# A two-layer graph attention and mixture-of-experts kernel: gate logits of 16 tiles as VectorE dots, a written engine order from the last attention block on, a guessed weight ring, and packing in half-megabyte pieces

## The chip, the core and the metric

The kernel runs on one core of one Trainium2 chip. The metric is the device time of one execution in microseconds. Each of the core's engines has a queue of its own: TensorE (PE in the profile, PEld for its weight loads), VectorE (DVE), ScalarE (ACT), GpSimd (POOL) and SyncE (SP). Most plain DMAs are issued from SP's queue; indirect DMAs (gathers and scatters by a list of row numbers) are issued from POOL's.

## The reference

There are 2708 tokens of 256 features, and an adjacency matrix of 2708 x 2708 integers of which some 1.2% are one. Two layers follow each other, each with a graph attention and a mixture of eight experts of which each token uses two. Cut to what matters:

```python
# layer 0
xn = layernorm(x)
q, k, v = xn @ Wq.T + bq, xn @ Wk.T + bk, xn @ Wv.T + bv
scores = where(adj > 0, q @ k.T / 16, -9e15)
x = x + elu(softmax(scores) @ v)
xt = layernorm(x)
top_p, top_idx = top_k(softmax(xt @ Wr + br), 2)
weights = top_p / top_p.sum(-1)
xe = layernorm(xt) * ln_g[e] + ln_b[e]            # for each expert e
y[e] = gelu(xe @ W1[e] + b1[e]) @ W2[e] + b2[e]   # hidden 1024
x = x + sum over the two experts of weights * y[e]
# layer 1: attention from s_src[i] + s_dst[j], the same mask, then eight experts of hidden 512
```

## The kernel before

**Tiles and blocks.** Tokens are cut into 22 tiles of 128 (the last has 20). The attention of layer 0 runs over six blocks of queries: five of 512 queries (tiles 0 to 3, 4 to 7 and so on) and a last one of 148 (tiles 20 and 21). A block has 22 key steps. In each, `scores` multiplies a tile of keys with the block's queries (L545; L552, L578 and L584 for the rest of the columns and the mask of the left-over keys), ScalarE takes the exponential (L557), and VectorE multiplies it with the mask (L560). Three key steps later (`LAG`), `attend` adds these weights times the values into four accumulators, one for each tile of the block (L609).

**Masks.** The mask of the next block is built during the present one: a quarter tile of the adjacency matrix is loaded on SP's queue, VectorE compares it (L411) and transposes it (L417). The columns of the left-over keys are loaded and compared by `load_apart` (compare L432), called at key step 14 (at step 0 in the last block). Its result, `apart`, is needed by the matmuls of L552 and L584 in the last key steps of the same block. At a block's end its mask is written to DRAM (`neighbours`, 1.4 MB), to be read again in layer 1.

**Routing beside the attention.** When a block's attends are done, `evict` (L634) copies the four accumulators out, and a generator `finish` for each tile goes to `line`. One step of each running generator is emitted per key step of the next block; a new tile starts every third key step (`line.gap`). `finish` divides by the softmax's sum, applies elu and adds the input, then `Experts.route` makes the tile's layernorm (its power on POOL, L257), and its gate: a normalised copy `xn` (L261), two transposes on TensorE (L274), a copy to `gT` on ScalarE, and a matmul with `wr` in four records (L1156), whose result VectorE adds to the bias. The two best experts follow, then a matmul that counts the tokens ahead of each one for its expert (L1188, L1189), and two indirect DMAs that write the tile's rows to `disp` in the order of the experts (L1207).

**Background DMAs.** `pack_weights` copies each expert's W1, W2 and biases into one row-packed array in DRAM. Its steps stand in a list `background`; one is issued on SP's queue at every fifth key step from block 1 on, and then, with the mask loads for layer 1, at every fifth slot of the experts.

**Experts of layer 0.** `experts0.run` works in 45 slots of 128 rows of one expert each. A slot gathers its rows (`fetch_rows`), takes the expert's packed weights from a ring of four buffers of 2.2 MB (`fetch_weights`, an indirect DMA on POOL, L1368, three slots ahead), turns the rows (`turned`), and does `up` (L1457, with gelu on ScalarE, L1465) and the `down` of the slot before (L1473; VectorE adds the weighted result, L1479). The first 24 slots take full groups of the first 16 tiles, so their first fetches (`experts0.begin`) are already issued at key step 5 of the last block. The tiles still in `line` are routed in the steps between `up` and `down`.

**Who sets the order.** In layer 0 and its experts, SP's queue keeps the order of the program. For the other engines a scheduler chooses the order of the instructions at build time from its estimates; `tc.issue_after` (at L1429 and L1448) holds the first slots' turning and bias behind the last block's eviction. Layer 1 and its experts already keep the program's order.

## Time and profile before

| | us |
|---|---|
| median of 3 runs | 1208.8 (1208.11 to 1211.92) |
| profiled execution | 1217.16 |
| its span | 1215.5 |
| mean granted TensorE clock | 0.982 |

Stages of the profiled execution, from a table of busy time by stretch:

| stage | stretch, us | TensorE busy, us | VectorE busy, us | ScalarE busy, us |
|---|---|---|---|---|
| start and block 0 | 0 to 124 | 112.96 | 69.30 | 34.52 |
| blocks 1 to 4 | 124 to 457 | 328.61 | 184.11 | 75.26 |
| last block | 457 to 501.6 | 43.27 | 25.79 | 10.09 |
| experts of layer 0 | 501.6 to 817 | 314.55 | 87.90 | 112.39 |
| attention of layer 1 | 817 to 963 | 140.73 | 96.72 | 90.17 |
| experts of layer 1 | 963 to 1190 | 205.26 | 89.22 | 109.48 |
| last sums and writes | 1190 to 1215.5 | 0.00 | 13.13 | 0.00 |

A profile line such as `L609 PE MATMUL acc<-v,p 128*128 128x257` names the source line, the engine, the operation, the tile that is written and those that are read, and the shapes. In a timeline the first column is the start from the span's beginning, the second the busy time; what stands in brackets is the idle time before the instruction on its engine, and what ended it. An `x4` joins four instructions in a row of one form. The granted clock is 1.00 at full TensorE clock and 0.5 at half.

### The profile page before, as it was taken

How to read it: one execution, taken by the hardware profiler on the slowest of the kernel's cores; microseconds unless marked ns; L12 is line 12 of the kernel's file. 1: busy time of each engine (PE TensorE's matmuls, PEld its weight loads, DVE VectorE, ACT ScalarE, POOL GpSimd, SP SyncE). 2: the span in 40 equal slices, each digit the busy share in tenths (PEclk: the TensorE clock that was granted, in tenths of full speed). 3: DMA queues.
4: the chain of work that ended last, by engine and by line, in shares of the span. 5: the costliest groups of instructions: out<-in, count | busy, mean ns of one | idle time of the engine just before them, and what ended most of it. 6: DMA issues, size and time to landing. Idle time of an engine off the chain costs nothing. (4 is left out here: it accounts for less than half of the span.)

```text
span 1215.5 us, 20794 instructions
## 1 busy us (share of the span) xinstructions
PE 1145.4 (94%) x6512; PEld 924.1 (76%) x6512; DVE 566.2 (47%) x2147; ACT 431.9 (36%) x1252; POOL 416.0 (34%) x519
## 2 busy tenths in 40 slices
PE   8989999999998999999999999998999988899990
PEld 5666666666665666789999999996999977789880
DVE  5466663754645647452222222224866776322224
ACT  3222221221212222353333333333776747444440
POOL 3011021110211213253333343334645558555540
PEclk9999999999998999899999999999999999999996
DMA  9394962999969394847677955633002427555557
GB/s 200 58 181 76 194 160 88 226 209 267 221 133 219 83 192 164 276 102 219 174 222 228 352 118 154 179 95 100 1 1 76 178 62 209 168 139 132 170 179 282
DMA packets 199628, 197.11 MB, mean 162 GB/s; under 512 B 91403, under 2 KB 183012, under 8 KB 193368
## 3 DMA queue, kind: packets, MB, share of 16 engines
q1 hardware_dynamic: 172442, 109.39, 40.6%
q0 software_dynamic: 26176, 83.56, 21.8%
q10 hardware_dynamic: 894, 2.77, 0.6%
q8 instruction: 54, 0.88, 0.3%
q14 instruction: 62, 0.51, 0.1%
HBM read 252.62 MB, written 66.15 MB: 262 GB/s over the span
## 5 line engine op out<-in xcount | busy, mean ns | idle before, releaser
L1457 PEld LDWEIGHTS mm<-xe,ring 128*128 128x128 f32 x2192 | 259.7, 194 | 26.0 <-issue 11.7
L1457 PE MATMUL mm<-xe,ring 128*128 128x128 f32 x2192 | 265.6, 278 | 14.5 <-DMA ring<-L_ffn_packed,weight_row 7.1
L1473 PE MATMUL acc<-ring,hT 128*128 128x256 f32 x1096 | 254.3, 381 | 1.1 <-issue 1.1
L1465 ACT ACTIVATE hT<-mm,ring 128x128 f32<-128x128 f32 x548 | 156.6, 370 | 273.1 <-issue 168.1
L1473 PEld LDWEIGHTS acc<-ring,hT 128*128 128x128 f32 x1096 | 201.3, 191 | 26.0 <-issue 2.3
L609 PEld LDWEIGHTS acc<-v,p 128*128 128x128 f32 (+1 forms) x880 | 159.7, 190 | 65.2 <-issue 41.0
L609 PE MATMUL acc<-v,p 128*128 128x257 f32 (+1 forms) x880 | 204.6, 384 | 2.3 <-DVE p L560 1.3
L545 PE MATMUL s<-g,xnT 128*128 128x512 f32 x420 | 203.0, 603 | 0.0
L1479 DVE SCALAR_TENSOR_TENSOR y<-acc,who,bias 128x256 f32<-128x256 f32 x92 | 44.4, 482 | 339.2 <-PE acc L1473 322.9
L257 POOL TENSOR_TENSOR ln_rs<-ln_rs,minus_half 128x2 f32<-128x2 f32 x88 | 66.0, 752 | 252.0 <-DVE ln_rs L253 214.4
L1207 POOL DMA_INDIRECT disp<-row,to x88 | 90.4, 1027 | 166.2 <-DVE to L1204 58.2
L1368 POOL DMA_INDIRECT ring<-L_ffn_packed,weight_row x92 | 97.6, 1060 | 128.3 <-PE acc L1473 88.4
L557 ACT ACTIVATE p<-s 128x512 f32<-128x512 f32 x105 | 62.5, 596 | 181.4 <-PE s L545 143.0
L854 PE MATMUL acc<-parts,m 128*128 128x266 f32 x924 | 126.2, 293 | 0.0
L854 PEld LDWEIGHTS acc<-parts,m 128*128 128x128 f32 x924 | 117.1, 185 | 4.1 <-ACT raw L881 0.9
L545 PEld LDWEIGHTS s<-g,xnT 128*128 128x128 f32 x420 | 76.6, 192 | 53.8 <-issue 50.5
L560 DVE SCALAR_TENSOR_TENSOR p<-p,mT 128x512 f32<-128x512 f32 x100 | 68.4, 686 | 95.2 <-ACT p L557 93.6
L1492 POOL DMA_INDIRECT xd<-y,who x45 | 71.8, 1595 | 118.7 <-issue 70.4
L821 ACT CAST m<-mT 128x512 fp32r<-128x512 fp8e4 (+4 forms) x168 | 71.6, 475 | 11.4 <-PE acc L854 7.0
L1485 POOL DMA_INDIRECT xd<-y,who x47 | 47.1, 1002 | 23.6 <-issue 11.0
L411 DVE TENSOR_SCALAR m_rows<-adj 128x512 fp8e4<-128x512 int32 (+1 forms) x105 | 42.1, 432 | 2.0 <-DMA adj<-in_adj_dram 1.9
L417 DVE STREAM_TRANSPOSE mT<-m_rows 128x128 int32<-128x128 int32 x100 | 33.4, 393 | 0.1
(252 smaller groups left out, 1028.3 us busy)
## 6 DMA issues: line engine op xcount, KB each, us to landing
adj<-in_adj_dram SPq DMA_DIRECT2D x100, 256.0 KB
L_ffn_packed<-in_L_ffn_W_dram SPq DMA_DIRECT2D x16, 1024.0 KB
xg<-disp SPq DMA_DIRECT2D x368, 32.0 KB
L_ffn_packed<-in_L_ffn_W_dram SPq DMA_DIRECT2D x16, 512.0 KB
neighbours<-mT SPq DMA_DIRECT2D x5, 1408.0 KB
mT<-neighbours SPq DMA_DIRECT2D x5, 1408.0 KB
xin<-in_x_dram SPq DMA_DIRECT2D x42, 128.0 KB
ring<-L_ffn_packed SPq DMA_DIRECT2D x4, 1154.0 KB
```

What stands on the lines that cost most here:

```text
L257: nc.gpsimd.tensor_tensor(rs[:r, 1], rs[:r, 0], minus_half[:r], ALU.pow)
L545: nc.tensor.matmul(ps[:kr, :nb], xnT[:, c, k0 : k0 + kr], g[:, c, :nb], start=(c == 0), stop=(c == DC - 1 and k < KEYS),)
L560: nc.vector.scalar_tensor_tensor(p, p, LARGEST, mask, op0=ALU.min, op1=ALU.mult)
L609: nc.tensor.matmul(accs[j][:r], p[keys, q0 : q0 + r], v[keys, k, :], start=(k == 0), stop=(k == NT - 1),)
L821: nc.scalar.copy(m[:, : q1 - q0], MASKS[b].of_key(mTs[b], k)[:, q0 - b * BN : q1 - b * BN],)
L854: nc.tensor.matmul(acc[:r], masks[t], parts[:, k, i], start=(k == 0 and i == 0), stop=False,)
L1207: nc.gpsimd.indirect_dma_start(disp[:], bass.IndirectOffsetOnAxis(ap=to[:r, j : j + 1], axis=0), rows2[:r, j], None,)
L1368: nc.gpsimd.indirect_dma_start(w, None, packed[:], bass.IndirectOffsetOnAxis(ap=self.weight_row[:, s : s + 1], axis=0), bounds_check=E * P ...
L1457: nc.tensor.matmul(ps[:, i, :], w[:, c * hidden + f * P : c * hidden + (f + 1) * P], xe[:, c, :], start=(c == 0), stop=(c == DC - 1),)
L1465: nc.scalar.activation(hT[:, f, :], ps[:, i, :], AF.Gelu, bias=w[:, b1 + f : b1 + f + 1])
L1473: nc.tensor.matmul(ps, hT[:, f, :], w[:, w2 + f * D : w2 + (f + 1) * D], start=(f == 0), stop=(f == hc - 1),)
L1492: start = nc.gpsimd.indirect_dma_start(xd[:], at, y, None, bounds_check=N - 1, oob_is_err=False, compute_op=ALU.add)
```

## The change

There are six parts.

1. **Gate by dots.** For tiles 0 to 15 the gate's logits are eight dot products of 256 on VectorE (`gate_dots`, four before and four after the normalisation of the row) with the centred gate columns `wr_rows`, built once in block 0 (`gate_rows`). They are scaled by the layernorm's factor and added to the bias in one instruction. `xn`, the transposes, `gT` and the gate's matmul remain for tiles 16 to 21.
2. **Written order.** From the beginning of the last block to the end of the experts of layer 0, TensorE, ScalarE and VectorE keep the order of the program (`order0`). `issue_after` falls away; a tile starts every fourth key step in the last block; two more `yield`s stand in `route`; the next slot's rows are turned before the `down` of the slot before.
3. **Guessed ring.** At key step 5 of the last block the first three ring buffers are loaded by plain DMAs with the weights of experts 0, 1 and 3; the steps of `begin` are spread over key steps 5, 10, 14 and 18. `fetch_weights` then reads only what differs from the guess.
4. **Packing in pieces.** The 16 packing steps become 32 of half a megabyte for layer 0 and 16 pairs for layer 1, one at every odd key step of blocks 1 to 4 and every odd slot.
5. **Left-over columns.** Their load moves to key step 4 of blocks 0 to 4; the compare stays at step 14.
6. **Memory.** `wdst_b` is loaded at the start of block 1 and not with the constants; the query and key weights live in a mask buffer during the preparation.

```diff
+    def gate_rows(raw):
+        raw = raw.rearrange("p (d e) -> p d e", e=E)
+        mean = small.tile([P, E], F32, name="gate_mean", bufs=1)
+        nc.vector.tensor_reduce(mean, raw.rearrange("p d e -> p e d"), AX.X, ALU.add)
+        nc.vector.tensor_scalar(mean, mean, 1.0 / D, None, ALU.mult)
+        nc.gpsimd.tensor_tensor(
+            wr_rows, raw.rearrange("p d e -> p e d"),
+            mean.unsqueeze(2).to_broadcast([P, E, D]), ALU.subtract,
+        )
+
+    def gate_dots(lg, x, r, experts, unused):
+        for e in experts:
+            nc.vector.scalar_tensor_tensor(
+                unused, x, 1.0, wr_rows[:r, e],
+                op0=ALU.mult, op1=ALU.mult, accum_out=lg[:r, e : e + 1],
+            )
...
+    def fold_gate(pool):
+        wdst_b = pool.tile([P, D], F32, name="wdst_b", bufs=1)
+        nc.sync.dma_start(wdst_b, a["L1_gnn_w_att"][D : 2 * D].partition_broadcast(P))
...
             for b, (b0, nb, ts_) in enumerate(BLOCKS):
+                if b == last:
+                    line.gap = GROUP
+                    order0.enter_context(
+                        tc.manual_schedule(engines={PE, Activation, DVE})
+                    )
...
-                    if k == (0 if b == last else NT - 8):
-                        apart = load_apart(b)
+                    if k == (0 if b == last else GROUP):
+                        apart_adj = load_apart(b)
+                    if k == NT - 8:
+                        apart = compare_apart(*apart_adj)
...
+                    if b == 0 and k == NT - 4:
+                        raw = wide.tile([P, BN // QUARTER, P], I32, name="adj", bufs=3)
...
+                        nc.sync.dma_start(
+                            raw, a["L0_ffn_Wr"].rearrange("d e -> (d e)").partition_broadcast(P)
+                        )
+                        gate_rows(raw)
...
-                    if background and b > 0 and k % 5 == 1 and (b > 1 or k > 10):
+                    if background and k % 2 == 1 and b < last and (b > 1 or (b == 1 and k > 10)):
                         background.pop(0)()
...
                     if b == last and k == LAG + 2:
-                        experts0.open()
-                        for _ in experts0.begin():
-                            pass
+                        n = FULL_AFTER[experts0.early]
+                        guess0 = experts0.open(
+                            [i * (n // RING) * E // (n + GROUP) for i in range(AHEAD)] + [-1]
+                        )
+                        for _ in range(AHEAD):
+                            next(guess0)
+                        begin0 = experts0.begin()
+                        for _ in range(6):
+                            next(begin0)
+                    if b == last and k in (LAG + 7, LAG + 11, LAG + 15):
+                        next(begin0)
...
         def route(self, t, x, logits=None):
             mean, once, twice, _ = norm_stats(x[:r], r)
+            by_dots = own_norm and t < self.early
+            if by_dots:
+                dots = small.tile([P, E], F32, name="dots")
+                gate_dots(dots, x[:r], r, range(E // 2), rows2[:r, 1, :D])
+                logits = dots[:r]
             yield
...
             if own_norm:
-                xt = rows.tile([P, D], F32, name="xn", bufs=4)[:r]
-                normed(xt, x[:r], mean, once)
                 normed(by_quarters(rows2[:r, 0, :D]), in_chunks(x[:r]), mean, twice)
+                if not by_dots:
+                    xt = rows.tile([P, D], F32, name="xn", bufs=4)[:r]
+                    normed(xt, x[:r], mean, once)
...
+                if by_dots:
+                    gate_dots(dots, x[:r], r, range(E // 2, E), rows2[:r, 1, :D])
                 nc.vector.tensor_copy(rows2[:r, 1, :D], rows2[:r, 0, :D])
...
             def slot(s, s1):
-                if own_norm:
-                    xe = turned(s)
                 after = turned(1) if s == 0 and not own_norm else None
-                hT, bias2 = up(w, xe, who[:, 1:2], own_norm and s < 2)
-                if s + 1 < s1 and not own_norm:
+                hT, bias2 = up(w, xe, who[:, 1:2])
+                if s + 1 < s1:
                     xe = after or turned(s + 1)
                 line.step()
...
-                if s % 5 == 4 and background:
+                if s % 2 == 1 and background:
                     background.pop(0)()
```

## Prediction

> **What bounds the kernel now.** I read the page's engine shares and its 40 slices first, to see whether one engine is full; then a table of stages, because the share is a mean over stages; then the TensorE timeline where the table shows idle time or a low clock; last the VectorE rows, because the change loads that engine.

> The page, engine shares and three of the slice rows:

> ```profile
> span 1215.5 us, 20794 instructions
> PE 1145.4 (94%) x6512; PEld 924.1 (76%) x6512; DVE 566.2 (47%) x2147; ACT 431.9 (36%) x1252; POOL 416.0 (34%) x519
> PE   8989999999998999999999999998999988899990
> DVE  5466663754645647452222222224866776322224
> PEclk9999999999998999899999999999999999999996
> ```

> TensorE carries the span, and every matmul taken from it is time, as long as nobody else becomes late. Each slice is 30.4 us; attention 0 is slices 1 to 16. The table of stages, for attention blocks 1 to 5 in halves (columns: stretch, length, busy PE, PEld, DVE, ACT, POOL, granted clock, DMA share, GB/s):

> ```profile
> 124.00:166.00 42.00, 42.00 (x165) 27.32 (x164) 29.02 (x111) 10.18 (x25) 6.40 (x15) 1.00 0.77 149
> 166.00:208.00 42.00, 42.00 (x187) 28.24 (x186) 19.20 (x68) 9.57 (x21) 6.18 (x6) 1.00 0.54 125
> 208.00:250.00 42.00, 42.00 (x162) 27.33 (x162) 28.53 (x105) 10.39 (x24) 5.29 (x12) 1.00 1.15 229
> 334.00:376.00 42.00, 38.98 (x161) 25.80 (x159) 22.42 (x74) 6.84 (x15) 7.81 (x11) 0.99 0.75 162
> 375.40:382.30 6.90, 6.27 (x16) 3.08 (x17) 1.13 (x4) 1.36 (x3) 0.00 (x0) 0.51 1.06 289
> 501.70:508.60 6.90, 6.90 (x34) 6.84 (x35) 3.88 (x26) 2.04 (x5) 0.00 (x0) 0.51 0.60 174
> 540.00:817.00 277.00, 277.00 (x1886) 258.31 (x1884) 63.59 (x201) 90.35 (x316) 102.30 (x77) 1.00 0.68 196
> ```

> TensorE has no idle time in most blocks nor in experts 0 (277.00 of 277.00). It idles at the end of block 3 (38.98 of 42), and two stretches ran at half clock. The TensorE timeline around the first of them, and a tile's gate inside block 1:

> ```profile
> 375.56 0.61 PE L552 MATMUL s<-minus_big,apart 128*128 128x128 bf16 x4 [3.02 <-DVE apart L432]
> 376.85 1.23 PE L609 MATMUL acc<-v,p 128*128 128x257 f32 x2 [0.47 <-ACT p L557]
> 377.87 5.80 PE L545 MATMUL s<-g,xnT 128*128 128x512 f32 x8
> ...
> 157.13 1.10 PE L545 MATMUL s<-g,xnT 128*128 128x512 f32 x2
> 158.15 0.44 PE L274 MATMUL misc<-ident,xn 128*128 128x128 f32 x2
> 158.42 1.90 PE L609 MATMUL acc<-v,p 128*128 128x257 f32 x8
> 160.16 0.51 PE L1156 MATMUL misc<-wr,gT 128*128 128x8 f32 x4
> 160.52 0.68 PE L545 MATMUL s<-g,xnT 128*128 128x512 f32 x1
> ```

> VectorE's timeline of two dots of the very form the change adds (256 wide, summed), made once in block 0, and its largest group in blocks 1 to 4:

> ```profile
> 36.01 0.42 DVE L212 SCALAR_TENSOR_TENSOR junk<-wfc,L_gnn_w_att_b 128x256 f32<-128x256 f32 x1
> 36.35 0.08 DVE L212 DVE_READ_ACCUMULATOR junk<-wfc,L_gnn_w_att_b 128x1 f32 x1
> 36.47 0.42 DVE L212 SCALAR_TENSOR_TENSOR junk<-wfc,L_gnn_w_att_b 128x256 f32<-128x256 f32 x1
> ...
> L560 DVE SCALAR_TENSOR_TENSOR p<-p,mT 128x512 f32<-128x512 f32 x80 | 55.1, 690 | 89.1 <-ACT p L557 87.5 <-issue 1.5
> ```

> **Gates of tiles 0 to 15: −10.1 us.** Durations overlap in the pipelined engine, so I take starts: the two transposes hold TensorE from 158.15 to 158.42, 0.27 us, the gate's four records from 160.16 to 160.52, 0.36 us. 16 × 0.63 = 10.1 us, all in stretches where TensorE has no idle time. The ScalarE copies that fall away (16) were on an engine at 10 of 42 us: nothing.

> **What VectorE pays for it: 128 dots.** Start to start 0.46 us: 59 us; 16 normalisations at 0.33 fall away: net +54 us, 13.5 per block. Block 1's halves stand at 29.0 and 19.2 of 42. The average fits (62 of 84). But the four tiles are routed mostly in the first half: 29.0 + 13.5 = 42.5 of 42, full. So the burst counts. I laid block by block the VectorE instructions between two L560 rows end to end, in the changed kernel's order, at the trace's starts (L560 0.60, other 256-wide 0.33 to 0.40, mask compare 0.36 and transpose 0.32, small ones 0.1), against 3.46 us of TensorE per key step (scores 1.73, attend 1.73). VectorE falls behind by at most 8.2, 7.1, 5.5 and 4.1 us in blocks 1 to 4, then catches up. TensorE first waits when the mask is over 9.1 us late: attend runs three key steps behind scores, 3 × 3.46 = 10.4, less the exponential (0.60) and the mask (0.69). Cover is thus 0.9 to 5 us, but the same reckoning for the old order came out up to 1 us short, and block 1 starts with two dots (L213) on a vector that is now loaded behind the 1.4 MB mask write (4.6 us at its 304 GB/s). The bounds are 0 and 12 us; I take +1.5, near the low end, since the reckoned peaks lie under the limit in all four blocks.

> [...]

> **Gate rows.** One reduction of 128x2048 on VectorE (eight times 0.33, 2.7 us), one POOL operation (eight times its 0.76 us addition of 128x256, 6.1 us) and 1 MB of DMA, at key step 18 of block 0. POOL and DMA idle there (slice 4: 0 tenths POOL), VectorE is at 6 of 10. Nothing; 2.7 us if VectorE were full.

> **The compare of the left-over columns: −7.1 us.** At block 3's end VectorE ran eight mask compares and their transposes (369.15 to 374.88) ahead of L432, and TensorE waited 3.02 us for it, then 0.47. The change loads these columns at step 4 instead of 14 and compares at 14; in the new VectorE order the compare precedes the attends of about step 11 to 14. Its DMA (0.3 MB, under 2 us at 200 GB/s) passes on SP's queue the mask loads of ten steps, for which VectorE waited 2.0 us in all: nothing. Also gone: 0.52 us of the same kind at block 2's end, and the half clock after the stall: 6.27 us of work at 0.51 instead of 1.00 is 3.1 us. 3.02 + 0.47 + 0.52 + 3.1 = 7.1. What is late next there is the exponential, by 0.5 us at most. Bounds: 0 (another instruction takes L432's place) and −7.1.

> That the clock goes with the stall is my reading of the rows: 375.4 follows 3.02 us of idle, and 501.7 only 0.98 us. [...]

> **Last block in written order, ring guessed: +2 us.** The scheduler fitted instructions to their due times; now TensorE, ScalarE and VectorE keep the program's order. Tiles 16 to 19 still pass TensorE. VectorE's work per four key steps is about 6.3 us, plus 0.9 of round trip to ScalarE, against 7.4 us of TensorE (steps are 1.7 to 1.9 us in this short block); it peaks 4.9 to 5.8 us behind where 5.65 is allowed. A VectorE instruction that waits for POOL's power (0.75 us) now holds all masks behind it, and on POOL that power stands behind the three ring fetches, each waiting for its guessed load of 2.23 MB to land. Moves of that size ran at about 410 GB/s in 479 to 491 (5.4 us each: no wait), SP's mask loads at about 200 GB/s (11 us each: 8 to 12 us of stall). So −1 (TensorE waits 0.78 us for a tile's normalisation at 518.1; the added step between may cover it) to +12; +2, nearer the fast row, which is of the same buffers. The half clock at 501.7 (3.4 us) I leave: the last sixteen attends and the eviction are as before. Gone, it gives another −3.4 and the 0.98.

> **Packing in 50 pieces instead of 16, and the order of experts 0: 0.** Some 5.5 MB of packing moves out of blocks 1 to 4, where the DMA share reaches 1.15, into experts 0, where it is 0.68; at 196 GB/s that is 28 us of engine time in 0.32 × 277 = 89 us free. TensorE's 7.0 us per slot hide it; if not, the ring's fourth load comes late. VectorE turns the next slot's rows a slot early and is at 63.6 of 277. Layer 1 is unchanged in order.

> **Sum.** −10.1 − 7.1 + 1.5 + 2 = −13.7 us. The profiled execution took 1217.16 (span 1215.5 and 1.7 around it) and would become 1203.5; it lay 8.4 above the median, 1208.8, so the forecast is 1195.1, said as 1195. With no new stall and the second half clock gone: −10.1 − 7.1 − 4.4 − 0.8 = −22.4, 1186.4. At the dear ends of both small terms short of a rival (+4, +6): 1201.6. Own range 1187 to 1202.

> **Rivals.** (1) VectorE becomes the bound in the bursts. For: the first halves are full (42.5 of 42), and other 256-wide forms of the same instruction take 479 ns (L302) against 420. A dot at 0.56 adds 3.2 us per block; with 2 to 3 us more of error the four blocks are 4.3 to 5.3, 3.2 to 4.2, 1.6 to 2.6 and 0.2 to 1.2 us late, 9.3 to 13.3. Three of these stops exceed 1 us and may bring a half clock of 3.1 each: 18.6 to 22.6 in all. −17.2 + 2 + that: 1212 to 1216. It decides from 18.8 us on. Against: mean load 74%. (2) The left-over compare, or an instruction in its place, still stalls: 1195 + 7.1 = 1202. (3) Written order and ring landing cost 8 to 12 instead of 2: −17.2 + 1.5 + 8 to 12, 1201 to 1205; with part of (2), 1207.

> **Chances.** Forecast 0.55, (1) 0.21, (2) 0.10, (3) 0.14. About 0.3%, 3.6 us, is what a measurement can tell from no change: bounds 1205.2 and 1212.4. Faster: 0.55 + 0.09 of (2) + 0.07 of (3) = 0.71. Same: 0.01 + 0.07 + 0.03 of (1) = 0.11. Slower: 0.18 of (1). The range leaves 0.02 below 1186 and 0.18 above 1212.

> **What would show it.** Right: no idle time on TensorE at the left-over columns, clock 1.00 through blocks 3 and 4, blocks about 2.5 us shorter, VectorE near 42 of 42 in their first halves, L560's wait for ScalarE much under 89 us. Wrong: idle time on TensorE with VectorE's L560 as releaser in blocks 1 to 3, idle time behind POOL's power or ring in the last block or first slots, or a half clock elsewhere.

## The result, and the profile after

The changed kernel took 1212.2 us (median of 14 runs, 1208.2 to 1217.1), the kernel before 1211.7 (14 runs): ratio 1.0006, interval 0.9990 to 1.0022. Nothing moved that can be measured, where 1195 was forecast. The median before now stands 2.9 us above the one of 3 runs from which the forecast started (1208.8). The page of the changed kernel, its span, engine shares and three slice rows:

```profile
span 1206.8 us, 20877 instructions
PE 1131.4 (94%) x6416; PEld 914.3 (76%) x6416; DVE 621.0 (51%) x2389; ACT 422.9 (35%) x1234; POOL 419.9 (35%) x524
PE   8989999999999998899999999998999998999990
DVE  5465992865856747652222222224866777322214
PEclk9999999999999998999999999999999999999995
```

TensorE is busy for 14 us less, and VectorE for 55 us more (54 was reckoned). The same table of stages as before (stretch, length, busy PE, PEld, DVE, ACT, POOL, clock, DMA share, GB/s):

```profile
124.00:166.00 42.00, 42.00 (x159) 27.24 (x158) 39.92 (x166) 9.83 (x25) 11.22 (x15) 1.00 0.67 141
208.00:250.00 42.00, 42.00 (x154) 27.07 (x153) 35.51 (x165) 9.90 (x24) 7.12 (x14) 1.00 0.95 216
250.00:292.00 42.00, 39.80 (x155) 24.96 (x154) 17.57 (x62) 7.69 (x15) 6.03 (x10) 0.96 0.63 157
334.00:376.00 42.00, 42.00 (x172) 26.47 (x171) 22.05 (x78) 8.57 (x17) 6.31 (x7) 1.00 0.76 201
540.00:817.00 277.00, 272.42 (x1858) 255.16 (x1857) 69.92 (x197) 88.94 (x312) 100.23 (x76) 1.00 0.74 209
```

The stop at block 3's end is gone (42.00 of 42 in 334 to 376), but idle time stands where there was none: in block 2 and in the experts (272.42 of 277). The TensorE timeline of the changed kernel gives the places (in its numbering L568 are the scores, L580 the exponential, L583 the mask, L632 the attends, L1512 the scaling of an expert's rows, L1533 `up`); these are its longer stops from block 1 to the end of the experts:

```profile
256.90 3.55 PE L568 MATMUL s<-g,xnT 128*128 128x512 f32 x4 [2.20 <-ACT p L580]
324.32 1.99 PE L568 MATMUL s<-g,xnT 128*128 128x512 f32 x4 [1.12 <-ACT p L580]
464.25 1.35 PE L568 MATMUL s<-g_last,xnT 128*128 128x148 f32 x4 [4.72 <-ACT p_last L580]
486.65 0.44 PE L294 MATMUL misc<-ident,xn 128*128 128x128 f32 x2 [1.16 <-DVE xn L281]
497.15 7.38 PE L1533 MATMUL mm<-xe,ring 128*128 128x128 f32 x64 [1.07 <-ACT raw L657]
509.10 3.96 PE L1533 MATMUL mm<-xe,ring 128*128 128x128 f32 x32 [1.11 <-DVE xe L1512]
611.04 3.87 PE L1533 MATMUL mm<-xe,ring 128*128 128x128 f32 x32 [1.43 <-DVE xe L1512]
699.12 3.87 PE L1533 MATMUL mm<-xe,ring 128*128 128x128 f32 x32 [2.62 <-DVE xe L1512]
```

Both kernels were profiled a second time. Lengths of stages, worked out from the traces (a block ends where the last copy of its accumulators starts, the experts where their last `down` matmul does):

| stage, us | before | before, again | changed | changed, again |
|---|---|---|---|---|
| start and block 0 | 134.7 | 135.0 | 132.8 | 133.6 |
| block 1 | 83.5 | 83.4 | 80.8 | 80.8 |
| block 2 | 81.7 | 81.7 | 82.5 | 82.5 |
| block 3 | 88.3 | 88.3 | 79.7 | 79.7 |
| block 4 | 75.6 | 75.5 | 73.2 | 73.2 |
| last block | 36.9 | 36.9 | 47.1 | 45.9 |
| experts of layer 0 | 325.0 | 326.0 | 326.2 | 326.1 |
| all after | 389.8 | 385.1 | 384.5 | 382.0 |

Blocks 0 to 4 gain 14 to 15 us, the last block gives 9 to 10 back, and the experts gain nothing although the half clock at their start (6.8 us long, 3.4 lost) is gone in one profile and half as long in the other. What follows the experts is the same program in both kernels, and varies by itself from one execution to the next.

### The profile page after: what moved, and what is told of

It is laid out like the page before. It is cut to its first block, busy times and chain, and to the rows that moved or that the text cites. A ratio compares the mean times of both kernels' runs of the same rounds, so it can differ in the third digit from the quotient of the medians.

```text
span 1206.8 us, 20877 instructions
## 1 busy us (share of the span) xinstructions
PE 1131.4 (94%) x6416; PEld 914.3 (76%) x6416; DVE 621.0 (51%) x2389; ACT 422.9 (35%) x1234; POOL 419.9 (35%) x524
## 3 DMA queue, kind: packets, MB, share of 16 engines
q10 hardware_dynamic: 894, 2.77, 0.6%
## 5 line engine op out<-in xcount | busy, mean ns | idle before, releaser
L1533 PEld LDWEIGHTS mm<-xe,ring 128*128 128x128 f32 x2192 | 259.1, 193 | 25.4 <-DVE xe L1512 7.8
L1533 PE MATMUL mm<-xe,ring 128*128 128x128 f32 x2192 | 262.9, 277 | 16.3 <-DMA ring<-L_ffn_packed,weight_row 7.7
L632 PEld LDWEIGHTS acc<-v,p 128*128 128x128 f32 (+1 forms) x880 | 160.0, 190 | 63.4 <-issue 37.5
L568 PE MATMUL s<-g,xnT 128*128 128x512 f32 x420 | 202.3, 601 | 3.3 <-ACT p L580 3.3
L632 PE MATMUL acc<-v,p 128*128 128x257 f32 (+1 forms) x880 | 204.2, 384 | 0.6 <-DVE p L583 0.6
L1555 DVE SCALAR_TENSOR_TENSOR y<-acc,who,bias 128x256 f32<-128x256 f32 x92 | 44.4, 482 | 267.3 <-PE acc L1549 264.6
L580 ACT ACTIVATE p<-s 128x512 f32<-128x512 f32 x105 | 62.0, 594 | 179.0 <-PE s L568 149.9
L568 PEld LDWEIGHTS s<-g,xnT 128*128 128x128 f32 x420 | 77.3, 191 | 56.1 <-issue 48.2
L583 DVE SCALAR_TENSOR_TENSOR p<-p,mT 128x512 f32<-128x512 f32 x100 | 72.3, 725 | 58.3 <-ACT p L580 58.1
L1512 DVE TENSOR_SCALAR xe<-xe_raw,ring 128x128 f32<-128x128 f32 x90 | 28.0, 360 | 65.7 <-DMA ring<-L_ffn_packed,weight_row 64.6
L1561 POOL DMA_INDIRECT xd<-y,who x47 | 46.9, 998 | 26.0 <-DVE y L1555 13.3
L261 DVE SCALAR_TENSOR_TENSOR row<-x,wr_rows 128x256 f32<-128x256 f32 x128 | 53.0, 416 | 0.3
```

The source lines that it names most:

```text
L568: nc.tensor.matmul(ps[:kr, :nb], xnT[:, c, k0 : k0 + kr], g[:, c, :nb], start=(c == 0), stop=(c == DC - 1 and k < KEYS),)
L583: nc.vector.scalar_tensor_tensor(p, p, LARGEST, mask, op0=ALU.min, op1=ALU.mult)
L632: nc.tensor.matmul(accs[j][:r], p[keys, q0 : q0 + r], v[keys, k, :], start=(k == 0), stop=(k == NT - 1),)
L1533: nc.tensor.matmul(ps[:, i, :], w[:, c * hidden + f * P : c * hidden + (f + 1) * P], xe[:, c, :], start=(c == 0), stop=(c == DC - 1),)
```

## Where the gain went: reading the trace

**ScalarE's queue.** In block 2 TensorE waits for an exponential (L580) that ScalarE could have done long before. First ScalarE's timeline, then VectorE's, of the changed kernel:

```profile
248.02 0.57 ACT L580 ACTIVATE p<-s 128x512 f32<-128x512 f32 x1
256.07 0.20 ACT L1261 ACTIVATE p<-p 128x2 f32<-128x2 f32 x1 [7.47 <-DVE p L1249]
256.18 0.19 ACT L1261 ACTIVATION_READ_ACCUMULATOR p<-p 128x1 f32 x1
256.27 1.06 ACT L580 ACTIVATE p<-s 128x512 f32<-128x512 f32 x2
```

```profile
252.15 0.46 DVE L455 TENSOR_SCALAR apart<-adj_rest 128x592 fp8e4<-128x592 int32 x1
...
253.47 0.68 DVE L583 SCALAR_TENSOR_TENSOR p<-p,mT 128x512 f32<-128x512 f32 x1
...
255.82 0.21 DVE L1249 TENSOR_SCALAR p<-best 128x8 f32<-128x8 f32 x1
```

A tile's two-expert softmax (L1261) stands ahead of the exponential in ScalarE's order and waits 7.47 us for VectorE, which is busy with dots. When it comes, ScalarE does two key steps' exponentials at once (x2): TensorE had filled both of its score buffers and stopped. The mask (L583) of the exponential of 248.02 came at 253.47, 4.9 us after it: VectorE is late, but TensorE isn't waiting for that. The compare of the left-over columns (L455) is at 252, in time.

**The placing of the first slots.** In the last block, ScalarE and VectorE of the changed kernel:

```profile
454.54 0.29 ACT L580 ACTIVATE p_last<-s 128x148 f32<-128x148 f32 x1 [1.40 <-PE s L568]
...
463.60 0.42 ACT L645 ACTIVATE neg<-neg 128x256 f32<-128x256 f32 x1 [7.26 <-DVE neg L644]
463.92 0.46 ACT L580 ACTIVATE p_last<-s 128x148 f32<-128x148 f32 x2
```

```profile
457.04 0.17 DVE L1305 COPY n_e<-misc 128x8 f32<-128x8 f32 x1 [1.18 <-DMA neighbours<-mT]
...
461.47 0.18 DVE L1394 SCALAR_TENSOR_TENSOR weight_row<-same,weights 128x24 int32<-128x24 f32 x1
461.57 0.30 DVE L583 SCALAR_TENSOR_TENSOR p_last<-p_last,mT_last 128x148 f32<-128x148 f32 x1
...
463.27 0.29 DVE L644 TENSOR_SCALAR neg<-raw 128x256 f32<-128x256 f32 x1
```

`begin` emits at one key step all that sorts the first slots: 20 small VectorE operations, 457.04 to 461.6, after a wait of 1.18 us. In written order the next tile's elu (L644, then L645 on ScalarE) is behind them, and the next exponential behind that. The same picture as in block 2, with 4.72 us of stop and a half clock of 6.8 us from 462.0 on, of which 4.6 us come after the stop (2.3 lost).

**The ring.** In the experts VectorE waits for weights:

```profile
610.64 0.60 DVE L1512 TENSOR_SCALAR xe<-xe_raw,ring 128x128 f32<-128x128 f32 x2 [6.78 <-DMA ring<-L_ffn_packed,weight_row]
698.72 0.60 DVE L1512 TENSOR_SCALAR xe<-xe_raw,ring 128x128 f32<-128x128 f32 x2 [7.98 <-DMA ring<-L_ffn_packed,weight_row]
```

The load for the slot at 611 was issued at 595.8 and landed at 610.6, 14.8 us for 2.2 MB; half a megabyte of packing had been issued at 593.3. My theory (L in the expectations): these three places eat the gain. The rivals: one profile is noise (V), VectorE as a whole is too late (also called V, in the runs a_spread and a_pegate), or the DMAs of the last block are late whatever the order (D).

## The experiments

All ratios are to the kernel before, with intervals.

**The changed kernel again** (no edit)

> The changed kernel, unaltered, for a second profile beside the first one. Theory L (the last block gives the gain back): the stops of its first profile come again at the same places: about 4.7 us at the exponential while VectorE works through the placing of the first slots (with a half clock after it), 1 to 2 us in blocks 2 and 3, and 5 to 6 us in the experts of layer 0. Theory V (noise of one profile): the stops move about, and the last block's is not there. Time: 1212, ratio to the kernel before 1.000, by both.

1212.1 us, 1.0004 (0.9986 to 1.0022). The stops in blocks 2 and 3 come again within 0.02 us (2.19, 1.11), the stop in the last block is 3.44 and the block takes 45.9, the stop at 697 is 2.77; that at 611 isn't there. V falls for all but that one.

**The kernel before again** (no edit)

> The kernel before, unaltered, for a second profile. If its stop at block 3's end is in most executions, it stands here again: 3.0 us of waiting for the compare of the left-over columns at about 372, and a half clock after it. If not, TensorE has no idle time there and the span is about 7 us shorter than in the first profile.

The TensorE timeline of the second profile:

```profile
375.83 0.61 PE L552 MATMUL s<-minus_big,apart 128*128 128x128 bf16 x4 [3.02 <-DVE apart L432]
```

The same stop, and a half clock of 6.8 us from 375.6: it belongs to the kernel.

**Gates on TensorE again**

```diff
-            by_dots = own_norm and t < self.early
+            by_dots = False
```

> The changed kernel, but the gates of all tiles go through TensorE again (the gate rows are still built in block 0, unused). Theory L: each gate costs TensorE 0.63 us where it had no idle time, and the small stops of blocks 2 and 3 (2.2 and 1.1 us, 1.7 of clock) go with the dots: 10.1 less 5.0, about 5 us slower than the changed kernel, ratio to the kernel before 1.004. Rival V (VectorE's bursts eat what the gates give): the same time as the changed kernel or faster, ratio 0.995 to 1.001.

1217.1 us, 1.0048 (1.0029 to 1.0066), 5.0 slower than the changed kernel measured beside it, as L had it. Block 1 is 83.3 for 80.8; block 2 is 80.9 for 82.5, without a stop.

**Routing every fourth key step**

```diff
-    line = Line(3)
+    line = Line(GROUP)
```

> The changed kernel, but a tile's routing starts every fourth key step in blocks 1 to 4 too, and not every third. If the stops of 2.2 us in block 2 (with its half clock of 3.4 us) and 1.1 us in block 3 come from VectorE's burst of dots, which makes ScalarE's queue wait: they go, 4 to 5 us faster than the changed kernel, ratio to the kernel before 0.996 to 0.997. Rival (they come from a power on POOL behind the scatters, not from the burst): they stay or move, ratio 0.999 to 1.001.

1207.3 us, 0.9972 (0.9954 to 0.9989). Block 2 falls from 82.5 to 79.0; its stop is 0.18 us, and no half clock follows; the stop of block 3 (1.15) stays. The time is 4 us under the changed kernel's, as expected, so the burst is the cause in block 2. That it acts through ScalarE's order is read from the timelines; that order alone wasn't changed. The table row of this kernel that answers to 250 to 292 above:

```profile
250.00:292.00 42.00, 42.00 (x172) 26.64 (x171) 20.53 (x71) 8.42 (x18) 6.99 (x9) 1.00 0.57 139
```

**The same with gates on TensorE** (both edits above)

> Routing every fourth key step and the gates of all tiles on TensorE again. What the dots are worth when VectorE's bursts are spread out: if TensorE's 0.63 us per tile is all, 8 to 10 us slower than the kernel with every fourth step and dots, ratio to the kernel before 1.003 to 1.006; if half of it is lost in the last block, where the start of the experts waits for something else, 4 to 5 us slower, ratio 1.000 to 1.002.

1215.1 us, 1.0051 (1.0025 to 1.0077), by the ratios 0.8% or 9.5 us slower than with dots, give or take 4 us by the two intervals. Blocks 1 to 4 take 320.0 against 312.5 in the traces, 7.5 us. Once the burst is spread, the dots are worth most or all of what the gates cost TensorE.

**Placing spread over key steps**

```diff
-                        for _ in range(6):
+                        for _ in range(2):
                             next(begin0)
-                    if b == last and k in (LAG + 7, LAG + 11, LAG + 15):
+                    if b == last and k in (*range(LAG + 3, LAG + 7), LAG + 8, LAG + 11, LAG + 15):
```

> The changed kernel, but the six steps of placing the first slots are spread over key steps 5, 6, 7, 8, 9 and 11 of the last block, instead of all at step 5. Theory L: the 4.7 us stop and the half clock after it (3.4 us) fall away, at most 1 us remains at each step: 6 to 8 us faster than the changed kernel, ratio to the kernel before 0.994 to 0.996. Rival V (VectorE as a whole is too late in the last block, the placing is only where it shows): the stop is cut into pieces of the same sum, ratio 0.999 to 1.001.

1214.6 us, 1.0030 (1.0016 to 1.0045): slower, where L had it 6 to 8 us faster. The 4.72 us stop is gone, the last block takes 44.4 and has no half clock; but other stops stand in its stead. TensorE's timeline of this kernel:

```profile
464.91 0.44 PE L294 MATMUL misc<-ident,xn 128*128 128x128 f32 x2 [1.53 <-DVE xn L281]
...
470.89 0.77 PE L568 MATMUL s<-g_last,xnT 128*128 128x148 f32 x4 [1.94 <-ACT p_last L580]
...
475.51 0.44 PE L294 MATMUL misc<-ident,xn 128*128 128x128 f32 x2 [1.16 <-DVE xn L281]
```

TensorE's idle time in the last block is 6.1 us in all, against 6.7 in the changed kernel and 0.5 in the kernel before. For the stops the rival of this run was right: they were cut into pieces of nearly the same sum, and only the half clock went. The first slot, besides, waits 6.44 us. VectorE's timeline:

```profile
499.22 0.45 DVE L1508 STREAM_TRANSPOSE xe_raw<-xg 128x256 f32<-128x256 f32 x1 [5.47 <-DMA xg<-disp]
```

The rows had been fetched at 467. What was late was the last block's mask write (issued 490.2, its packets done at 498.5), whose DMA lies among 2.2 MB for the fourth ring buffer, fetched at 489.2; the changed kernel fetched it at 461.9.

**Spread, and the fourth buffer fetched first**

```diff
+            fourth = []
             if self.own_norm:
+                fourth.append(self.fetch_weights(AHEAD))
                 yield
...
+                if s == AHEAD - 1:
+                    self.weights += fourth
```

> The changed kernel with the placing spread over key steps 5 to 11, and the fourth ring buffer fetched ahead of the first three, as it was in the changed kernel. If the 6.4 us at the experts' start of the spread kernel came from that fetch being late (2.2 MB at 489 us, which delays the mask's write whose buffer the experts take over): it goes, last block 44 us, 4 to 5 us faster than the spread kernel, 2 to 3 faster than the changed one, ratio to the kernel before 0.997 to 0.999. If not: 1.003 as the spread kernel.

1210.8 us, 0.9995 (0.9979 to 1.0012). The 6.4 us wait is gone (1.07 as in the changed kernel), the mask's write done at 492.4. The two edits together bring 1 us, which the intervals don't tell from none, and not 2 to 3: the last block still takes 44.5.

**No guess**

```diff
-                        guess0 = experts0.open([...] + [-1])
-                        for _ in range(AHEAD):
-                            next(guess0)
+                        experts0.open()
```

> The changed kernel, but the ring is not loaded by a guess: its first three buffers come by the indirect DMAs of key steps 10, 14 and 18. Theory L (the placing of the first slots is what stops the last block): that stop stays, 4 to 5 us, and the first slots wait for their weights, 0 to 6 us more: ratio to the kernel before 1.000 to 1.005. Rival G (the guessed loads hold SP's queue and the DMA engines, and the last block waits for that): the last block gets 5 us shorter, ratio 0.995 to 0.998.

1215.5 us, 1.0047 (1.0024 to 1.0071), 5 us slower than the changed kernel: the stop in the last block is 3.97, the first slot waits 3.96. The guess is a gain; G falls.

**The scheduler's order**

```diff
-                    order0.enter_context(tc.manual_schedule(engines={PE, Activation, DVE}))
```

> The changed kernel, but TensorE, ScalarE and VectorE keep the scheduler's order throughout layer 0 (no written order). Theory L: the stop in the last block goes since the scheduler puts masks between the small operations, and the first slots start as before: 6 to 9 us faster than the changed kernel, ratio to the kernel before 0.993 to 0.996. Rival (the written order is worth something later, the stops in the experts come from late ring loads, which the order does not touch): the last block wins 6 to 8 us, the first slots lose 3 to 6, ratio 0.997 to 1.000.

1213.6 us, 1.0011 (0.9991 to 1.0030). The last block falls to 37.8 with 0.9 us of idle time in it, and 10.1 us pass before the experts start: what the written order costs in the block it saves, within the interval, at its end. L had 6 to 9 us faster and falls.

**Parts 2 and 3 undone together**

> The changed kernel with parts 2 and 3 undone together (the scheduler's order in the last block and the experts, no guess, the first fetches all at key step 5, as before); dots, early left-over columns and packing in pieces stay. Theory L (parts 2 and 3 give back what the blocks gain): the last block takes 37 to 39 us and not 46, no stop at the experts' start: 7 to 9 us faster than the changed kernel, ratio to the kernel before 0.992 to 0.995. Theory D (once blocks 1 to 4 are shorter, the DMAs of the last block are late whatever the order; that is what held the kernels with the old packing up by 20 to 27 us at the first slot): a stop of 5 us or more at the experts' start, ratio 1.000 to 1.010.

1215.4 us, 1.0039 (1.0024 to 1.0055). The last block takes 40.3, and then TensorE waits:

```profile
501.31 2.47 PE L1518 MATMUL mm<-xe,ring 128*128 128x128 f32 x10 [11.87 <-DMA who<-disp]
```

L was wrong here: these parts are worth about 4 us on the whole, D right. All four ring loads (8.9 MB) are issued at 466 to 475, and the row fetches of SP among them crawl: SP needs 10.7 us (483.8 to 494.5) for one slot's four, and the last mask's write stands behind them at 496.6.

**The last mask written from ScalarE's queue**

```diff
+                if b == last:
+                    nc.scalar.dma_start(neighbours[b][:].bitcast(F32), mT.bitcast(F32))
```

> The kernel with parts 2 and 3 undone, but the last block's mask is written from ScalarE's DMA queue and not from SP's. If its 11.9 us at the experts' start is the mask's write, held up on SP's queue behind row fetches (issued at 496.6 us, 8 us after the last block's end, the experts start 2.5 us after it lands, and take over its buffer): the stop shrinks to 2 to 4 us, 8 to 10 us faster than that kernel, ratio to the kernel before 0.995 to 0.997. Rival (the rows of the first slot themselves land late): the stop stays, ratio 1.004.

1213.5 us, 1.0022 (1.0007 to 1.0037): 2 us better, which the two intervals don't tell from none, and not 8 to 10. ScalarE issued the write only at 494.3, when SP's held-up row fetches went on as well; the wait moved into the block. Neither queue alone is what holds it; that both wait for row fetches that land behind the ring's loads is argued from these times, not shown.

**Packing as before**

> The changed kernel, but with the packing as before (16 whole steps, at every fifth key step and every fifth slot). Theory L: the stops of 2.8 us near 697 and 1.4 us near 611, where the rows' scaling waits for the ring's load to land, come from the pieces at every odd slot, and go: 3 to 5 us faster than the changed kernel, ratio to the kernel before 0.996 to 0.998. Rival (the stops come from the three slots' order, not from the pieces): they stay, ratio 1.000.

1229.4 us, 1.0144 (1.0116 to 1.0171), against every theory. The experts take 322.3, and of their late stops one of 0.66 remains; but the last block takes 69.8, with stops of 13.6 and 8.8 us and the clock at half for 31 us. SP's timeline of this kernel, and after it the same place in the changed one:

```profile
411.27 0.62 SPq L447 DMA_DIRECT2D adj_rest<-in_adj_dram  x1
436.25 0.32 SPq L418 DMA_DIRECT2D adj<-in_adj_dram  x1
```

```profile
393.32 0.61 SPq L447 DMA_DIRECT2D adj_rest<-in_adj_dram  x1
412.01 0.33 SPq L418 DMA_DIRECT2D adj<-in_adj_dram  x1
```

SP waits 24 us for a load of the last block's mask, and 18 in the changed kernel, but there from 394 on. After it four whole packing steps go out at 443 to 467 (421 to 447 in the kernel before), two of them behind the last block's start at 449.6.

**The left-over columns alone, on the kernel before**

> The kernel before with part 5 alone (left-over columns loaded at key step 4, compared at 14). If the stop of 3.0 us at block 3's end and its half clock are in most executions of the kernel before: 6 to 7 us faster, ratio 0.994 to 0.996. If they are in few: 0 to 3 us, ratio 0.998 to 1.000.

1226.4 us, 1.0120 (1.0095 to 1.0145): slower by 15, where 6 to 7 us faster was expected. Block 3 gains its 6.4 us, blocks 0 to 4 together 11; the last block takes 48.5 and the first slot then waits 20 us. TensorE's and SP's timelines of this kernel:

```profile
521.64 3.75 PE L1460 MATMUL mm<-xe,ring 128*128 128x128 f32 x16 [20.15 <-DMA who<-disp]
```

```profile
418.13 0.35 SPq L402 DMA_DIRECT2D adj<-in_adj_dram  x1
418.52 0.61 SPq L427 DMA_DIRECT2D adj_rest<-in_adj_dram  x1
437.93 0.32 SPq L398 DMA_DIRECT2D adj<-in_adj_dram  x1
```

Behind the left-over columns SP waits 19 us for the next mask load; before it went on at 417.65 without a gap. All that is behind on SP's queue comes later, four whole packing steps among it: the mask write at 469.3 (456.2 before), the first rows at 497.7 (476.4). Why that load waited (its buffer is freed by VectorE, whose order the scheduler had changed) wasn't tried. It goes on at 437.9, as in the run before (436.2), though the dots, which shorten the blocks, are not in this kernel.

**Dots and left-over columns alone, on the kernel before** (parts 1, 5 and 6)

> The kernel before with parts 1, 5 and 6 alone (dots for 16 tiles, the left-over columns loaded early, the memory that these need); order, ring and packing as before. Theory L (written order with the guessed ring, and the packing in pieces, give the gain back in the last block and in the experts): the blocks 1 to 4 gain about 13 us over the profile of before, nothing is given back: ratio to the kernel before 0.990 to 0.994. Rival B (the profile of before was a slow one, the stop at the left-over columns and its half clock are not in most executions, so only some 5 us are there to be had): ratio 0.995 to 0.997.

1230.6 us, 1.0154 (1.0130 to 1.0179), 19 us slower, where both theories had a gain. Blocks 1 to 4 take 316.1 against 329.0: a gain of 12.9. The last block takes 43.3 and the experts start 28.1 us after it.

**Background pieces in quiet slots**

```diff
-                if s % 2 == 1 and background:
+                if s in (1, 2, 3, 4, 8, 9, 10, 11, 15, 16, 20, 21, 28, 29, 30, 33, 38) and background:
```

> The changed kernel, but the background pieces in the experts at the slots in which the ring loads little, instead of at every odd slot. If the stops of 1.4 to 2.8 us near 610 and 697 come from a piece or a mask load that shares the DMA engines with the ring: both go, the experts take 321 us and not 325, 4 to 6 us faster (3.4 us more where a half clock followed), ratio to the kernel before 0.995 to 0.998. Rival (the ring's own 2 MB a slot is too much there): they stay, 1.000.

1203.1 us, 0.9953 (0.9935 to 0.9970). 6 us under the changed kernel by the ratios. Both stops go, the experts take 321.4 (326.2 and 326.1 in the changed kernel); from the table of stages of this kernel:

```profile
540.00:812.00 272.00, 272.00 (x1863) 256.01 (x1862) 70.94 (x200) 88.94 (x312) 100.44 (x76) 1.00 0.73 210
```

So the pieces at every odd slot were what made the ring late.

**All four edits** (every fourth key step, placing spread, fourth buffer first, quiet slots)

> The changed kernel with four edits: routing every fourth key step in all blocks, the placing spread over key steps 5 to 11, the fourth ring buffer fetched first, and the background pieces in the experts moved to slots in which the ring loads little (1 to 4, 8 to 11, 15, 16, 20, 21, 28 to 30, 33, 38). If the give-back is the sum of these places: gap 4 us, the placing 3 us, the ring's late loads 4 us: 8 to 11 us faster than the changed kernel, ratio to the kernel before 0.990 to 0.994. If they hide one another: as routing every fourth step alone, 0.997.

1199.1 us, 0.9925 (0.9901 to 0.9948): faster than both kernels. The edits apart gave 0.32% (every fourth step), 0.09% (placing) and 0.51% (quiet slots) over the changed kernel, 0.92% in sum; together 0.79%.

## Why the prediction was wrong

**Gates, right.** −10.1 was said; block 1 shortened by 2.6 and block 4 by 2.3 to 2.4, and the dots are worth 7.5 us in the traces and 9.5 ± 4 in the times once the burst is spread.

**Left-over columns, right in size, wrong as a part by itself.** −7.1 was said for block 3's end. The block shortened by 8.6, of which 2.5 are gates and 1.1 was lost to a new stop: −7.2. The half clock went with the stall: the changed kernel ran at full clock from 260.6 to 462.0. Wrong by itself: alone on the kernel before, this part cost 15 us, in the last block and at the experts' start.

**VectorE's bursts, the failing step in the blocks.** I took +1.5, with cover of 9.1 us until TensorE waits for a mask. VectorE's lateness was not what failed: 35.5 to 39.9 of 42 us in the first halves (42.5 said), and a mask 4.9 us late where TensorE stopped, in a block for which 7.1 was reckoned. The wrong number is the cover. It counted TensorE and VectorE alone. ScalarE also keeps an order, with small activations of the routing in it that wait for VectorE, and TensorE has only two score buffers in this program: it stops some two key steps after the exponential is held up. The cost was 2.2 and 1.1 us of stop, 1.7 of clock and 1.0 in three small waits at the selections: 6.0.

**Last block, +2 said, 9 to 10 measured: the second failing step.** Here too the release goes through ScalarE, and my sum of VectorE's work (6.3 us per four key steps) left out the placing, 4.5 us in one step. That is where the longest stop stood, but it isn't the whole cost: with the placing spread out TensorE still idles 6.1 us, waiting in the written order for a tile's normalised copy (1.2 to 1.5 us each) and for one exponential, and the block takes 44.5 for 36.9. With the scheduler's order it takes 37.8. How much of the rest is the placing's work and how much the order's wasn't separated. The range of −1 to +12 held the cost; rival (3) named the right place and the wrong cause: the guessed loads, which I feared, are worth 5 us. Rival (1)'s 1212 to 1216 holds the measured time by luck: it had the loss in blocks 1 to 4, which gained.

**Packing, 0 said (for 48 pieces, not 50): wrong twice.** Free DMA time in the mean (0.32 of 277 us) didn't protect a ring load in the slot in which a piece fell: the edit of slots alone is worth 6 us (0.51%), 4.7 of them in the traces' experts. And without the pieces the kernel loses 17, in the last block: SP's queue is held up until 436.2, and the old whole steps behind it fall beside the last block's own loads. That the shorter blocks alone do this isn't shown, as the same wait stands in the kernel without the dots. My reckoning went by stages of the trace of before, which doesn't show what a moved load holds up behind it.

**The sum.** −10.1 − 7.2 + 6.0 + 9.5 and about 0 in the experts is −2; the traces' layer 0 shows −3.4 and −5.1, as block 0, which the sum leaves out, is 1.4 to 1.9 shorter, and blocks 1 to 4 gain 12.9 for the sum's 11.3. The medians have +0.5 ± 2. Part of the rest may be the clock: (1 − granted clock) × span is 24.8 us in the median of 12 executions of the changed kernel and 23.0 in 33 of the kernel before, while the time less this is 1187.1 and 1189.1. That would be two us less of work and stops, and two more of half clock; but in the 14 first executions of the changed kernel the same figure is 26.6, so it moves as much without any change, and in the profiled executions some 12 us of it lie behind TensorE's last matmul, where they cost nothing. The last 2 us between profiles and medians stay open.

## What to carry to other kernels

A slack reckoned between two engines holds only if the path between them goes through no third queue that may wait (ScalarE's waited 7.47 us for VectorE, and TensorE 2.20 us behind it): follow the release instruction by instruction, and count what stands ahead of it on each queue. Where a stage hides a chain (fetches, placing, weights) behind its length, shortening the stage is no gain until that chain starts earlier (parts 1, 5 and 6 alone made blocks 1 to 4 12.9 us shorter and the kernel 19 us slower), so cost a change's parts together, and look in the next stage for what the shorter one was hiding. A background transfer belongs in the slots whose own loads are small, however much is free in the mean (the choice of slots alone was worth 6 us, with a mean DMA share of 0.74 before it and 0.73 after).

## What was not expected of the hardware

A half clock followed short stops. In the changed kernel it began at 257.2, right after the 2.20 us stop that ended at 256.90, and lasted 3.4 us; all seven profiles with this stop of 2.2 us show it, within 1.4 us of its end, and with 0.18 us of stop (every fourth step) or 1.21 (parts 2 and 3 undone) there is none. The stop of 1.1 us in block 3 was not followed by one in any profile.

The length of the stop doesn't decide alone. The stop of 2.62 us that ended at 699.12 was followed by no half clock, the one of 2.77 us at 697.29 in the second profile by 3.4 us of it (columns as above, the granted clock third from the end; first the changed kernel, then its second profile):

```profile
694.08:697.49 3.41, 2.41 (x12) 1.78 (x10) 0.00 (x0) 0.14 (x1) 1.98 (x2) 1.00 0.99 374
697.49:700.91 3.42, 1.79 (x15) 1.79 (x16) 2.12 (x7) 0.00 (x0) 0.28 (x1) 1.00 0.50 77
700.91:704.32 3.41, 3.41 (x26) 3.25 (x25) 0.23 (x1) 2.28 (x8) 2.34 (x2) 1.00 0.53 125
```

```profile
695.40:698.82 3.42, 1.53 (x13) 1.53 (x14) 1.86 (x6) 0.00 (x0) 0.13 (x1) 1.00 0.49 70
698.82:702.23 3.41, 3.41 (x18) 3.41 (x18) 0.45 (x2) 1.14 (x4) 2.49 (x2) 0.50 0.78 228
```

Such losses also move between executions of one kernel: in the kernel before, (1 − clock) × span ran from 18.1 to 26.7 us over 33 executions, and it goes with the time (correlation 0.81).
